# Norm's root and reciprocal on four rows instead of 128, spread by way of DRAM a slot later, its sum in another PSUM bank, and the x taps of the convolution a slot later

## The chip, the core and the metric

The kernel runs on one core of one Trainium2 chip. The metric is the device time of one execution in microseconds. The engines are named as in the profile: PE is TensorE (PEld its weight loads), DVE is VectorE, ACT is ScalarE, POOL is GpSimd, SP is SyncE, whose queue issues the DMAs.

## The reference, cut to what matters

A layer norm is followed by a Mamba-2 mixer and, beside it, a linear layer with mixture-of-LoRA; both are added to the input. There are 2048 tokens of 1024 features, 64 heads of 64 channels in 8 groups of 512 channels, and a state of 128. Everything is fp32. The change concerns the norm of the mixer (`var` and `yn`) and the convolution before it.

```python
proj = jnp.einsum('bld,pd->blp', hidden_states, in_proj_w)   # gate, hbc, dt
for k in range(K):                                           # K = 4
    conv = conv + pad[:, k:k + L, :] * conv_weight[:, k]
xBC = silu(conv)                                             # x, Bm, Cm
...                                                          # scan over tokens gives y
yg = y.reshape(B, L, G, GROUP_SIZE)                          # 8 groups of 512 channels
var = jnp.mean(yg * yg, axis=-1, keepdims=True)
yn = (yg * lax.rsqrt(var + EPS)).reshape(B, L, I) * norm_weight
yn = yn * silu(gate)
out = jnp.einsum('bli,di->bld', yn, out_proj_w)
```

## The kernel before, in words

Channels lie on the 128 partitions and tokens along the free axis. The work has two stages on one stream of instructions for each engine.

The first stage, up to about 2700 us, interleaves the input projections with the scan. A projection is computed in pairs of channel tiles by a Strassen-like scheme of seven products (`pair`, L450): product 1 goes to bank `pa`, 6 to `px`, 5 to `py`, then 2, 7, 3 and 4 add to them. Each product is four matmuls of 128x128 weights with 512 tokens, which the profile records as eight passes, since an fp32 matmul is two. DVE or ACT evicts what is finished (L474 to L482 and `stored`, L523): for a gate tile, ACT applies Silu to what DVE evicted (L533). Products of the x tiles are named ps_a_x, ps_x_x, ps_y_x in the profile, those of the gate ps_a_g and so on. In order they are here called products one to seven of a pair. The four banks of the pool `proj` hold them; the four banks `y`, `e`, `st` and `aux` (`ps_one`) hold everything else.

The scan is cut into 32 blocks (s, g, half): s is a half of 1024 tokens, g a group of 512 channels, half one of two runs of 512 tokens. A block has four slots c = 0 to 3 of 128 tokens. In each slot the main loop runs four or five products and, between them, what the scan needs:

- `scan_b` for this slot: ps_y (scores times `xdt`), ps_e (state times C), ps_st (the product that updates the state, from `xdd`); then on DVE ecp (L763), y (L764) and the state addition (L778), which needs POOL's multiplication of the state (L83).
- `scan_a` for the next slot, in three steps: the decay scan es on DVE (L688); ps_cb and a transpose into bank aux, copied by ACT (cbm, bt) and multiplied on DVE (dab, L702); four transposes ps_xt into bank aux, from which ACT makes eight pieces of `xdt` (L713) and eight of `xdd` (L721).
- `conv` for the next block in slots c = 1 and 2: ACT writes the first tap (L640), DVE adds three more taps for each of six tiles of 512 tokens (L646), first the two tiles `bc`, then the four tiles `xg`; ACT applies Silu (L653). `xg` has two buffers. The next block's `xg` takes the buffer of the block before this one, so it waits until that block's normed y has been stored.
- the norm of the block before, in slot c = 0: `norm_mean` sums the squares over channels with one matmul against a 128x128 tile of ones, so all 128 partitions hold the same sum; it writes bank aux (ps_nv) and ACT takes the root (L813). `norm_gate` takes the reciprocal (L819), scales four tiles by it (L822), multiplies them with the gate (L830), and SP stores them (y, L831). The squares come from `norm_squares` in slot c = 3 of the block itself.
- in the first half, `small`: the layer norm, the decays dt and the router of the second half's tokens, in small DVE steps (L311 to L395); `at` (L329) goes to an exp on ACT (L330).

The lists `parts[0]` to `parts[4]` spread side steps over the products of a slot. PE's order, the pieces of xdt and xdd, and Silu of the convolution are kept as written. The rest is put into each engine's queue by the framework's scheduler, so DVE's order differs from the order of the source. Each engine then runs its queue in order, and SP too: a DMA that waits holds up those behind it.

The second stage, from about 2742 us, is the output projection, in the same manner with two levels; the change does not touch it.

Of the kernel before, what the change touches and what calls it, by code (L numbers as in the profile page):

```python
# [8 lines left out]
F32 = mybir.dt.float32  # L9
AF = mybir.ActivationFunctionType  # L10
# [17 lines left out]
P = 128  # L28
TS = 1024
NS = L // TS  # L30
TB = 512
Q = 128
NQ = TB // Q
# [9 lines left out]
def mamba_lora_kernel(  # L43
# [17 lines left out]
    nc = tc.nc  # L61

    dram = ctx.enter_context(tc.tile_pool(name="dram", bufs=1, space=bass.MemoryType.DRAM))
    const = ctx.enter_context(tc.tile_pool(name="const", bufs=1))
# [6 lines left out]
    ps_one = ctx.enter_context(tc.tile_pool(name="ps_one", bufs=1, space=bass.MemoryType.PSUM))  # L71
    scan_ctx = ExitStack()
    p1 = scan_ctx.enter_context(tc.tile_pool(name="p1", bufs=1))
# [4 lines left out]
    def mm(*args, **kw):  # L78
        tc.keep_in_program_order(nc.tensor.matmul(*args, **kw))  # L79
# [11 lines left out]
    ones = const.tile([P, P], F32, name="ones")  # L91
    nc.vector.memset(ones, 1.0)
    ident = const.tile([P, P], F32, name="ident")
    make_identity(nc, ident)
    eps = const.tile([P, 1], F32, name="eps")
    nc.vector.memset(eps, EPS)


# [42 lines left out]
    nw = p1.tile([P, INNER // P], F32, name="nw")  # L141
# [151 lines left out]
    def small_mm(ps, x_of):  # L293
        for k in range(KT):
            mm(ps, x_of(k), wsm[:, k, :], start=(k == 0), stop=(k == KT - 1))
# [295 lines left out]
    def products(n, side):  # L591

        nonlocal done
        left = list(side)
        for i in range(n):
            next(stream)
            done += 1
            take = -(-len(left) // (n - i))
            for step in left[:take]:
                step()  # L600
            left = left[take:]
        for step in left:
            step()

    def steps(gen, n):

        return [lambda: next(gen, None) for _ in range(n)]


    xbc_of = {}  # L610
# [174 lines left out]
    def load_gate(s, g, half):  # L785
        sg = p1.tile([P, 4, TB], F32, tag="sg", name=f"sg_{s}_{g}_{half}")
        at = s * TS + half * TB
        nc.sync.dma_start(sg, gate_d[g][:, :, at : at + TB])
        sg_of[s, g, half] = sg

    norm_of = {}
# [14 lines left out]
        yield  # L806

    def norm_mean(s, g, half):
        y = y_of[s, g, half]
        ps = ps_one.tile([P, TB], F32, tag="aux", name=f"ps_nv_{s}_{g}_{half}")  # L810
        mm(ps, ones, y[:, 0, :], start=True, stop=True)
        std = p1.tile([P, TB], F32, tag="rms", name=f"rms_{s}_{g}_{half}")
        nc.scalar.activation(std, ps, AF.Sqrt, bias=eps, scale=1.0 / (4 * P))  # L813
        norm_of[s, g, half] = std

    def norm_gate(s, g, half):

        xg, std = xbc_of[s, g, half][0], norm_of[s, g, half]
        nc.vector.reciprocal(std, std)  # L819
        yield  # L820
        for j in range(4):
            nc.vector.scalar_tensor_tensor(  # L822
                xg[:, j, :], xg[:, j, :], nw[:, 4 * g + j : 4 * g + j + 1], std,
                ALU.mult, ALU.mult,
            )
        yield
        at = s * TS + half * TB
        for j in (0, 2):
            two = xg[:, j : j + 2, :]
            nc.vector.tensor_tensor(two, two, sg_of[s, g, half][:, j : j + 2, :], ALU.mult)  # L830
            nc.sync.dma_start(y_d[g][:, j : j + 2, at : at + TB], two)  # L831
            yield
# [121 lines left out]
    blocks = [(s, g, h) for s in range(NS) for g in range(G) for h in range(2)]  # L954
# [15 lines left out]
    def target(slot):  # L970
        for (s0, p0), (s1, p1_) in zip(plan, plan[1:]):
            if slot <= s1:
                return p0 + (p1_ - p0) * (slot - s0) // (s1 - s0)
# [4 lines left out]
    for b, blk in enumerate(blocks):  # L978
        s, g, half = blk
        prev = blocks[b - 1] if b else None  # L980
        nxt = blocks[b + 1] if b + 1 < len(blocks) else None

        i, stage = divmod(b - 2, 3)
        piece, after = (1, i), stage
        if not (s == 0 and 0 <= i < NQ):
            piece = after = None
        if b == 14:
            ln_ctx.close()
            wo_ctx = ExitStack()
            wo = wo_ctx.enter_context(tc.tile_pool(name="wo", bufs=1, reuse_waits="tile"))  # L990
        if b == 15:
            base_left = left_sums
        if 0 <= b - 15 < 16:
            left_sums = out_sums(wo, b - 15)
        for c in range(NQ):
            slot += 1
            n = target(slot) - done
            follow = (*blk, c + 1) if c + 1 < NQ else (*nxt, 0) if nxt else None
            second = (*blk, c + 2) if c + 2 < NQ else (*nxt, c + 2 - NQ) if nxt else None
            side = []  # L1000
            if c == 0 and nxt:
                side += [lambda: load_raw(*nxt)]
            if after == 0 and c == 1:
                load_piece(*piece, "sg", p1)
                ln = ln_next(*piece)
            if after == 0 and c == 2:
                side += steps(ln, 3)
            if after == 0 and c == 3:
                side += steps(ln, 4)
            if after == 1 and c in (0, 2, 3):  # L1010
                side += steps(rest, 1)
            if c in (1, 2) and nxt:
                if c == 1:
                    conv_steps = conv(*nxt)
                side += steps(conv_steps, 4)
            if c == 2 and after != 0:
                side += [lambda: load_gate(*blk)]
            if b == 1 and c < 2:

                js = range(4) if c == 0 else range(4, 7)  # L1020
                side[:0] = [
                    lambda j=j: nc.sync.dma_start(xop_d[0][j], ops_of["x", 0][j]) for j in js
                ]
            a = scan_a(*follow) if follow else iter(())
            parts = [side[i * len(side) // n : (i + 1) * len(side) // n] for i in range(n)]

            products(1, parts[0])
            if c == 0 and prev:
                norm_mean(*prev)
            scan_b(*blk, c)  # L1030
            if b == 14 and c:
                next(left_sums)
            if 0 <= b - 15 < 16 and c:
                next(left_sums)
            if second:
                load_decays(*second)
            next(a, None)
            if c == 0 and prev:
                out = norm_gate(*prev)
                parts[1:4] = [[*p, lambda: next(out, None)] for p in parts[1:4]]  # L1040
                parts[3] += [lambda: next(out, None)] * 2
            if c == NQ - 1:
                sq = norm_squares(*blk)
                parts[1] += steps(sq, 2)
                parts[2] += steps(sq, 1)
            products(1, parts[1])
            next(a, None)
            products(1, parts[2])
            products(1, parts[3])
            next(a, None)  # L1050
            if after == 0 and c == 1:
                next(ln)
            for i in range(4, n):
                products(1, parts[i])
            if b == 14:
                left_sums = base_sums(wo, c)
                next(left_sums)
            if 0 <= b - 15 < 16 and c == 0:
                if b == 15:
                    next(base_left)  # L1060
                next(left_sums)
            if after == 0 and c == 2:
                next(ln)
            if after == 0 and c == 3:
                sm = lp.tile([P, 2, NSM], F32, tag="sm", name=f"sm_{piece[0]}_{piece[1]}")
                ps = ps_one.tile([P, 2, NSM], F32, tag="st", name=f"ps_sm_{piece[1]}")
                for h in range(2):
                    small_mm(ps[:, h, :], lambda k: piece_of[piece][:, k, h, :])
                nc.scalar.copy(sm, ps)
                rest = small(*piece, slice(piece[1], 2 * NQ, NQ), sm, home)  # L1070
                load_gate(*blk)
            if (after, c) in ((1, 1), (2, 0)):
                next(rest)
    norm_mean(*blocks[-1])
    for _ in norm_gate(*blocks[-1]):
        pass
    wo_ctx.close()
# [156 lines left out]
    for t, (s, p) in enumerate(passes):  # L1234
        last = t + 1 == len(passes)
        for u, i in enumerate(units):
            ops, next_ops = next_ops, {}
            side = [[] for _ in range(7)]
# [87 lines left out]
            for n, j in enumerate(inner):  # L1326
                w = w_ready.pop(0)
                ps = {1: pa, 2: pa, 6: px, 7: px, 4: px, 5: py, 3: py}[j]
                for q in range(2):
                    for k in range(KH):  # L1330
                        mm(
                            ps[:, q, :], w[:, q, k, :], ops[j][:, k, :],
                            start=(n < 3 and q + k == 0), stop=(k == KH - 1), skip_group_check=True,
# [69 lines left out]
```

## Time and profile before

| what | us |
|---|---|
| time, median of 3 runs (3449.82 to 3451.58) | 3449.89 |
| the profiled execution's own time | 3453.59 |
| its span | 3451.8 |
| PE busy | 3409.2 |
| DVE busy | 2501.2 |
| ACT busy | 1164.7 |
| POOL busy | 696.1 |

The span runs from the first to the last instruction of the program in the profiled execution; 1.8 us of its own time lie around it. Busy time is a sum over all stages. A busy PE is not always a PE at its full rate: passes are pipelined, and a pass that starts late or runs at a lower clock counts as busy too. So the rate is read from the distance between starts of passes: 0.43 us for 512 columns, 0.109 for 128 columns (ps_xt). In the lines of groups and of the timeline, out<-in are the program's own names and x is a count; the bracket or the last column tells how long the engine sat idle just before and what ended it.

### The profile page before, as it was taken

Reading aid. Unit: us, or ns where it says so; the run is one execution under the profiler, and the core shown is the slowest. Engines: PE = TensorE matmul, PEld = TensorE weight load, DVE = VectorE, ACT = ScalarE, POOL = GpSimd, SP = SyncE. Lnnn points to the kernel's source line nnn. Section 1 sums busy time; section 2 is a strip of 40 time slices with the busy share of each in tenths; the row PEclk is TensorE's granted clock in tenths of the full one; section 3 lists DMA queues with packets and bytes.
Section 4 is the critical chain, followed back from the end, with each engine's and each line's share of the span. In section 5 each row is a group of like instructions: output and inputs, shape, how many; then the busy total and the mean of one; then the engine's idle time right before and its main releaser. Section 6 shows DMA issues by size and latency. Waiting matters only on the chain.

```text
span 3451.8 us, 38274 instructions
## 1 busy us (share of the span) xinstructions
PE 3409.2 (99%) x12818; PEld 1992.3 (58%) x12818; DVE 2501.2 (72%) x2861; ACT 1164.7 (34%) x3182; POOL 696.1 (20%) x443
## 2 busy tenths in 40 slices
PE   9999999999999999999999999999999999999999
PEld 7444544544545544454455445444444588888888
DVE  7548877877977877777787877777775466566665
ACT  2234453444444443444445444444442100000000
POOL 3122223222222211322223232222321000000000
PEclk9999999999999999999999999999999999999999
DMA  6546655655666676887778887777778687586654
GB/s 235 186 166 197 205 191 186 211 187 197 203 200 204 205 254 219 291 256 231 236 242 260 236 258 244 245 237 236 228 239 267 243 277 242 196 299 188 214 164 146
DMA packets 530324, 769.83 MB, mean 223 GB/s; under 512 B 35152, under 2 KB 264656, under 8 KB 527440
## 3 DMA queue, kind: packets, MB, share of 16 engines
q1 hardware_dynamic: 530128, 767.39, 68.7%
q8 instruction: 102, 1.67, 0.2%
q14 instruction: 94, 0.77, 0.1%
HBM read 516.64 MB, written 250.61 MB: 222 GB/s over the span
## 4 chain that ended last, share of the span: by engine, by line
PE 84%; DVE 9%; issue 3%; ACT 2%; DMA 1%; POOL 0%; SPq 0%; DVEq 0%; ACTq 0%; POOLq 0%
PE ps_x_x L79 12%; PE ps_x_w L79 8%; PE ps_a_x L79 8%; PE ps_y_x L79 8%; PE ps_x_g L79 7%; PE ps_a_w L79 6%; PE ps_y_w L79 6%; PE ps_y_g L79 5%; PE ps_a_g L79 4%; PE ps_y L79 3%; PE ps_e L79 3%; PE ps_st L79 2%; PE ps_x_b L79 2%; DVE xg L646 2%; PE ps_a_b L79 2%
## 5 line engine op out<-in xcount | busy, mean ns | idle before, releaser
L83 POOL TENSOR_TENSOR state<-state,tot 128x512 f32<-128x512 f32 x112 | 153.7, 1373 | 1326.0 <-PE ps_e L79 1199.8
L688 DVE TENSOR_TENSOR_SCAN es<-dab,here 128x1024 f32<-128x1024 f32 x128 | 304.6, 2380 | 83.4 <-ACT xdd L721 81.8
L646 DVE SCALAR_TENSOR_TENSOR xg<-rawx,cw,xg 128x512 f32<-128x512 f32 x384 | 339.2, 933 | 18.7 <-ACT xg L640 18.0
L79 PE MATMUL ps_x_w<-t,w 128*128 128x256 f32 x1344 | 303.8, 379 | 0.0
L713 ACT ACTIVATE xdt<-ps_xt,dt 128x64 f32<-128x64 f32 x1024 | 223.8, 333 | 209.7 <-PE ps_xt L88 209.7
L79 PEld LDWEIGHTS ps_x_w<-t,w 128*128 128x128 f32 x1344 | 255.4, 190 | 41.5 <-issue 7.7
L721 ACT ACTIVATE xdd<-xdt,es 128x64 f32<-128x64 f32 x1024 | 261.9, 388 | 0.0
L1340 ACT COPY s<-ps_a_w 128x512 f32<-128x512 f32 x28 | 16.4, 586 | 636.0 <-PE ps_a_w L79 555.5
L83 POOL TENSOR_TENSOR wo<-wo 128x512 f32<-128x512 f32 (+1 forms) x112 | 213.4, 1906 | 6.8
L79 PE MATMUL ps_a_w<-q,w 128*128 128x256 f32 x896 | 202.5, 379 | 0.0
L702 DVE TENSOR_TENSOR dab<-es,cbm 128x1024 f32<-128x1024 f32 x128 | 180.1, 1407 | 29.6 <-ACT cbm L698 29.6
L79 PEld LDWEIGHTS ps_a_w<-q,w 128*128 128x128 f32 x896 | 170.2, 190 | 23.6 <-issue 0.5
L79 PEld LDWEIGHTS ps_y<-dab,xdt 128*64 128x64 f32 x2048 | 114.6, 139 | 105.1 <-ACT xdd L721 38.7
L79 PE MATMUL ps_x_x<-op_again,s_x 128*128 128x512 f32 x384 | 172.7, 592 | 0.0
L79 PE MATMUL ps_y_x<-op_again,s_x 128*128 128x512 f32 x384 | 172.7, 592 | 0.0
L79 PE MATMUL ps_a_x<-op_again,a_x 128*128 128x512 f32 x384 | 172.7, 592 | 0.0
L79 PE MATMUL ps_x_x<-op,s_x 128*128 128x512 f32 x368 | 165.5, 592 | 0.0
L79 PE MATMUL ps_y_x<-op,s_x 128*128 128x512 f32 x368 | 165.5, 592 | 0.0
L79 PE MATMUL ps_a_x<-op,a_x 128*128 128x512 f32 x368 | 165.4, 592 | 0.0
L79 PE MATMUL ps_y<-dab,xdt 128*64 128x128 f32 x2048 | 146.6, 284 | 7.8 <-ACT xdt L713 7.8
L531 DVE TENSOR_TENSOR ev<-ps_x_x,s_x 128x512 f32<-128x512 f32 x94 | 64.5, 687 | 120.5 <-PE ps_x_x L79 116.1
L646 DVE SCALAR_TENSOR_TENSOR bc<-rawb,cw,bc 128x512 f32<-128x512 f32 x192 | 145.7, 790 | 1.9 <-ACT bc L640 1.0
(236 smaller groups left out, 6118.6 us busy)
## 6 DMA issues: line engine op xcount, KB each, us to landing
w<-w SPq DMA_DIRECT2D x196, 512.0 KB, 3.7
dab<-da_d SPq DMA_DIRECT2D x128, 512.0 KB, 5.5
raw<-ev SPq DMA_DIRECT2D x192, 256.0 KB, 3.3
a_x<-in_w_in_dram SPq DMA_DIRECT2D x168, 256.0 KB, 4.2
w<-wo SPq DMA_DIRECT2D x96, 448.0 KB, 4.3
ecp<-run_d SPq DMA_DIRECT2D x256, 128.0 KB, 4.0
gate<-ev SPq DMA_DIRECT2D x128, 256.0 KB, 3.9
sg<-gate SPq DMA_DIRECT2D x32, 1024.0 KB, 7.8
```

The source lines that it names most:

```text
L79: tc.keep_in_program_order(nc.tensor.matmul(*args, **kw))
L83: ins = nc.gpsimd.tensor_tensor(*args)
L531: nc.vector.tensor_tensor(e, ps, add, alu)
L646: nc.vector.scalar_tensor_tensor(dst[:, i, :], raw[:, i, k : k + TB], cw[:, ti, k : k + 1], dst[:, i, :], ALU.mult, ALU.add,)
L688: nc.vector.tensor_tensor_scan(es.rearrange("p h t -> p (h t)"), dab.rearrange("p h t -> p (h t)"), here, 0.0, ALU.mult, ALU.add,)
L702: nc.vector.tensor_tensor(ms, es, cbm.unsqueeze(1).to_broadcast([P, HG, Q]), ALU.mult)
L713: ins = nc.scalar.activation(xdt[:, h, :], x_t[:, h, :], AF.Copy, scale=dt_of[s][:, half * NQ + c, at : at + 1],)
L721: ins = nc.scalar.activation(xdd[:, h, :], xdt[:, h, :], AF.Copy, scale=es[:, h, Q - 1 : Q])
L1340: nc.scalar.copy(s1, pa)
```

## The change

- `norm_mean` sums into bank st instead of aux, with four matmuls instead of one. Each has 128 tokens, and as weights four columns of a new tile `row_of` [128, 8], which is zero but for column 3 (ones) and column 7 (EPS). Matmul c takes columns 3 - c to 6 - c, so its sums land in row c of a tile [4, 128], and the other three rows get zeros added. ACT takes the root of 4x128 instead of 128x512.
- A new step `norm_spread` takes the reciprocal of 4x128, stores it to DRAM, and loads it back with one DMA that copies the row of 512 to all 128 partitions.
- `norm_mean` moves behind `scan_b` and the second product of slot c = 0, `norm_spread` stands behind the third product, and `norm_gate` moves to slot c = 1.
- Of the convolution's steps, two instead of four stand in slot c = 1 (the tiles bc) and five instead of four in slot c = 2 (the tiles xg).
- After the last block the same steps follow each other with nothing between.

```diff
-    eps = const.tile([P, 1], F32, name="eps")
+    row_of = const.tile([P, 8], F32, name="row_of")
+    nc.vector.memset(row_of, 0.0)
+    nc.vector.memset(row_of[:, NQ - 1 : NQ], 1.0)
+    eps = row_of[:, 7:8]
     nc.vector.memset(eps, EPS)
...
     def norm_mean(s, g, half):
         y = y_of[s, g, half]
-        ps = ps_one.tile([P, TB], F32, tag="aux", name=f"ps_nv_{s}_{g}_{half}")
-        mm(ps, ones, y[:, 0, :], start=True, stop=True)
-        std = p1.tile([P, TB], F32, tag="rms", name=f"rms_{s}_{g}_{half}")
-        nc.scalar.activation(std, ps, AF.Sqrt, bias=eps, scale=1.0 / (4 * P))
-        norm_of[s, g, half] = std
+        n = f"{s}_{g}_{half}"
+        ps = ps_one.tile([NQ, Q], F32, tag="st", name=f"ps_nv_{n}")
+        for c in range(NQ):
+            mm(
+                ps, row_of[:, NQ - 1 - c : 2 * NQ - 1 - c], y[:, 0, c * Q : (c + 1) * Q],
+                start=(c == 0), stop=(c == NQ - 1),
+            )
+        rms = p1.tile([P, TB], F32, tag="rms", name=f"rms_{n}")
+        nc.scalar.activation(
+            rms[0:NQ, 0:Q], ps, AF.Sqrt, bias=eps[0:NQ], scale=1.0 / (4 * P)
+        )
+        norm_of[s, g, half] = rms
+
+    def norm_spread(s, g, half):
+        rms = norm_of[s, g, half]
+        std = rms[0:NQ, 0:Q]
+        n = f"{s}_{g}_{half}"
+        nc.vector.reciprocal(std, std)
+        std_d = dram.tile([NQ, Q], F32, tag=f"std_d_{n}", name=f"std_d_{n}")
+        nc.sync.dma_start(std_d, std)
+        nc.sync.dma_start(
+            rms, std_d.rearrange("c t -> (c t)").unsqueeze(0).to_broadcast([P, TB])
+        )

     def norm_gate(s, g, half):
-        xg, std = xbc_of[s, g, half][0], norm_of[s, g, half]
-        nc.vector.reciprocal(std, std)
-        yield
+        xg, rms = xbc_of[s, g, half][0], norm_of[s, g, half]
         for j in range(4):
             nc.vector.scalar_tensor_tensor(
-                xg[:, j, :], xg[:, j, :], nw[:, 4 * g + j : 4 * g + j + 1], std,
+                xg[:, j, :], xg[:, j, :], nw[:, 4 * g + j : 4 * g + j + 1], rms,
                 ALU.mult, ALU.mult,
             )
...
-                side += steps(conv_steps, 4)
+                side += steps(conv_steps, 2 if c == 1 else 5)
...
             products(1, parts[0])
-            if c == 0 and prev:
-                norm_mean(*prev)
             scan_b(*blk, c)
...
-            if c == 0 and prev:
+            if c == 1 and prev:
                 out = norm_gate(*prev)
-                parts[1:4] = [[*p, lambda: next(out, None)] for p in parts[1:4]]
-                parts[3] += [lambda: next(out, None)] * 2
+                for i in range(1, 4):
+                    parts[i] += steps(out, 1)
...
             products(1, parts[1])
+            if c == 0 and prev:
+                norm_mean(*prev)
             next(a, None)
             products(1, parts[2])
+            if c == 0 and prev:
+                norm_spread(*prev)
             products(1, parts[3])
...
     norm_mean(*blocks[-1])
+    norm_spread(*blocks[-1])
     for _ in norm_gate(*blocks[-1]):
         pass
```

## The prediction

> **What bounds the kernel now.** I read the page first (busy shares, slices, chain), then the list of what TensorE waits for, then the timeline around its longest wait, then busy time in the four slots of one block, and last the rows of the operations that change. From the page:
>
> ```profile
> span 3451.8 us, 38274 instructions
> PE 3409.2 (99%) x12818; PEld 1992.3 (58%) x12818; DVE 2501.2 (72%) x2861; ACT 1164.7 (34%) x3182; POOL 696.1 (20%) x443
> ```
>
> TensorE is the bound: 99% busy in every slice. So the change can win only what TensorE still waits for. Those waits, engine, line and cause, then us in total, times and longest:
>
> ```profile
> PE ps_nv L79 <- ACT xdt L713: 10.5, 4, 3.3
> PE ps_y L79 <- ACT xdt L713: 7.8, 5, 4.6
> ...
> PE ps_x_x L79 <- DVE ev L531: 2.8, 3, 1.3
> PE ps_x_g L79 <- DVE ev L531: 2.5, 5, 0.9
> ...
> PE ps_st L79 <- ACT xdd L721: 1.4, 4, 0.4
> ```
>
> All named waits sum to 37.3 us (1.1% of the span); the five shown make 25.0, and each lies in the scan, where the change works. A wait also costs what comes after it. The longest one (start, length, what, and in brackets the idle time before it):
>
> ```profile
> 443.47 3.60 PE L79 MATMUL ps_x_g<-op,s_g 128*128 128x512 f32 x8
> 451.65 2.17 PE L79 MATMUL ps_y<-dab,xdt 128*64 128x128 f32 x16 [4.58 <-ACT xdt L713]
> 453.75 1.76 PE L79 MATMUL ps_e<-bc,state 128*128 128x128 f32 x8
> 455.34 1.02 PE L79 MATMUL ps_st<-xdd,bt 128*128 128x512 f32 x2
> ```
>
> Elsewhere ps_y follows its product at once and goes to ps_e after 1.03 us, ps_e to ps_st after 0.97 (1552.33, 1553.36, 1554.35). Here it is 2.10 and 1.59: the clock granted between 451.65 and 455.34 was 0.54.
>
> Who is behind it? VectorE's queue. Busy time in slots c = 0 to 3 of block (1,4,1), one row each: window, its length, then PE, PEld, DVE, ACT, POOL:
>
> ```profile
> 2172.00:2192.00 20.00, 20.00 (x65) 9.63 (x65) 15.76 (x17) 7.91 (x24) 1.04 (x1) 1.00 0.53 168
> 2192.00:2210.00 18.00, 18.00 (x79) 9.28 (x73) 16.02 (x21) 9.17 (x26) 7.70 (x5) 1.00 0.71 218
> 2210.00:2228.00 18.00, 18.00 (x73) 9.29 (x69) 8.48 (x9) 5.82 (x21) 10.72 (x5) 1.00 1.01 328
> 2228.00:2246.00 18.00, 18.00 (x72) 9.37 (x71) 15.79 (x19) 10.64 (x26) 0.00 (x0) 1.00 0.85 249
> ```
>
> VectorE is 15.8 and 16.0 us busy in c = 0 and 1, 8.5 in c = 2, 15.8 in c = 3. An eviction that stands behind such a queue is late, ScalarE stands in order behind the eviction, xdt behind that, and TensorE behind xdt. The change empties c = 0 and fills c = 2.
>
> **What the Trainium skill says.** "TensorE: Matmul & The Clock Gate", Part 1: an array idle for about 3.4 us falls to half clock and needs as long to come back. The trace agrees: 0.54 granted after the 4.58 us wait. [...] the quickest stores here (s_b_d below) land after 2.0. "SBUF — State Buffer", Who interferes with whom: a VectorE instruction with two SBUF inputs contends with a GpSimd one that reads SBUF. The taps agree: 0.74 us alone, 1.75 beside GpSimd's work (1970 to 1973).
>
> **The change part by part.** Rows used (VectorE and ScalarE: ns min/median/max; DMA: KB and median us to landing):
>
> ```profile
> L822 DVE SCALAR_TENSOR_TENSOR xg<-xg,nw,rms x128: 736/745/1750, 270.1 to 2700.6; 128x512 f32<-128x512 f32 x128
> L813 ACT ACTIVATE rms<-ps_nv,eps x32: 687/687/689, 261.9 to 2694.5; 128x512 f32<-128x512 f32 x32
> L819 DVE RECIPROCAL rms<-rms x32: 3341/3346/3354, 264.0 to 2695.2; 128x512 f32<-128x512 f32 x32
> dab<-da_d SPq DMA_DIRECT2D x128, 512.0 KB, 5.5
> ecp<-run_d SPq DMA_DIRECT2D x256, 128.0 KB, 4.0
> s_b_d<-wb SPq DMA_DIRECT2D x16, 256.0 KB, 2.0
> ```
>
> 1. Reciprocal. 32 of 3.35 us go. The new one has 128 columns; 128x512 takes 3.35 and 128x256 1.75, so 6.25 ns a column gives 0.95. Saved: 32 x 2.4 = 77 us of VectorE, none of it on TensorE's path by itself. ScalarE's root falls from 0.69 to about 0.3 (cbm, 128 columns, takes 0.26), and 8 of 91 table loads (1.28 each) go by the new order: no path.
>
> 2. The sum on TensorE. Two passes of 512 columns, start to start 0.43 + 0.52 = 0.95 a block, become eight of 128 columns; ps_xt's, as long, start 0.109 apart: 0.87. Only four output rows are used, which no row shows. Bounds: 0.1 less each (-3 us in all) to 0.2 more (+6; ps_y and ps_e pay some 0.2 between them when the array's shape changes). I take +1.
>
> 3. The sum moves behind the state product and a projection product, from bank aux to bank st. Before, it needed aux, so all eight xdt; now ps_y comes first and needs only the first xdt, and ps_st all eight xdd. Where it waited, ps_st can start 0.1 after xdd's end, less the 0.95 that the sum then costs later:
>  - wait at 1573.15: xdd ends 1574.98, ps_st began 1577.65: 2.67 - 0.1 - 0.95 = 1.6;
>  - at 2168.03 and 2471.99: 2.83 - 1.05 = 1.8 each;
>  - at 2320.52: 1.25 - 1.05 = 0.2.
>  Sum 5.4 us. The other 27 blocks had no such wait and gain nothing.
>  New wait: the sum on bank st needs the state addition (L778) to have read ps_st. Before, the reciprocal stood ahead of it, typically 0.81 to 4.15 us after ps_st began, the addition ending at 5.3. In the changed order it follows ecp directly: it ends 1.5 us after the old place of ps_st, the sum comes at -0.95 + 0.86 + 3.44 = 3.35. Margin 1.8; least where es ends late (0.9). Only block (0,2,1), with ecp at 3.2, misses it: 1 us. Behind a waiting sum stand ps_cb and the next product. GpSimd's order is unchanged, and its state multiplication ends by 2.0.
>
> 4. The small head's steps. In four slots (waits at 446, 701, 951, 1199) ScalarE's exp of `at` stands ahead of xdt, and `at` behind the reciprocal, four scalings (0.75) and two gate products (1.22): 8.8 us. In the new order at (L329) stands ahead of all scaling. From the product's last pass to ps_st takes 2.52 when undisturbed; it took 8.86, 4.97, 4.58 and 4.97. Gain 6.3 + 2.45 + 2.05 + 2.45 = 13.3 us. Next late there would be the eviction of product five, which now follows the scaling; it has two products of room.
>
> 5. Taps (L646) a slot later. In the new order four of the eight evictions that TensorE waited for stand ahead of the taps; the waits at 1607 (1.1), 1974 (1.5), 2350 (0.85) and 2507 (1.1 and 1.1 behind it) go: 5.6 us. 2126 has one tap more ahead of it: +0.7.
>  Cost: VectorE in c = 2 rises from 8.5 by eight to twelve taps (0.74 to 1.75): 15 to 20 of 18 us; c = 0 falls to about 8, c = 1 to about 13. In c = 3 there are 2 us of room. I take 4 us of new late evictions; bounds 0 and 40.
>
> 6. The way through DRAM. SP gets 64 more issues (0.35 each), and the load waits for the store: behind it stand weight loads and ev's stores, for up to 2 us a block. SP has idle stretches (2181.3 to 2184.4), weights come a pair of products ahead: nothing. Trip: store 2.2, issue, load between ecp's and dab's, 4.5: rms is there 9.8 us after the sum began. VectorE stands in order before the first scaling for some 3 us, then needs 5.4 for it. In seven blocks the eviction of product five is behind that and is due 18.9 after the sum began: 9.8 + 5.4 + 0.7 = 15.9 is in time. I take 2 us; bounds 0 and 25. The convolution's first step waits for y's store (3.1) to free xg; it had 20 us of room.
>
> 7. The end. The last block's scaling has no slot to move into: the trip ends scaling some 3 us later (2706.8), and the s_b_2 eviction behind it is due 2708.0. I take 0.5; bounds 0 and 3.
>
> Sum: 5.4 + 13.3 + 5.6 = 24.3 won; 1 + 1 + 0.7 + 4 + 2 + 0.5 = 9.2 lost; -15 us. The profiled execution's own time is 3453.59: 3438.5. The median of the runs is 3.7 lower, and the waits are the same instructions there: 3449.9 - 15 = 3435.
>
> **Rivals.** (a) The waits only move: a full c = 2 gives as many late evictions as go. For it: DMA share 1.01 and GpSimd 10.7 us in that very slot. Lost 9 + 13: 3448. (b) Slower: VectorE becomes the bound in c = 2. With GpSimd at work a tap takes 1.75; if the twelve average over 1.0 us, they exceed c = 2's 9.5 and c = 3's 2 free us. At 1.25 they spill 3.5 us into the evictions at the end of c = 3, on which xdt waits; in 12 of the second half's 16 blocks that is 42 lost: 3449.9 - 24 + 5 + 42 = 3473; at 1.15 (2.3 us, 28 lost), 3459. Against: many taps are still placed in c = 1, which has 5 us of room. (c) No new waits: 3449.9 - 24.3 + 1.5 = 3427. (d) The row's load lands later than 7.5 us (state<-st, also a load of what was just stored, 7.4): product five's eviction late in seven blocks, +10: 3445.
>
> **Chances.** My forecast 0.58 (3427 to 3443), (a) and (d) 0.20, (b) 0.14, (c) 0.08. About 0.2% (7 us) is what measurement can tell from no change. Faster: 0.95 x 0.58 + 0.08 + 0.2 x 0.20 = 0.67; slower 0.13; same 0.20. The range leaves a tenth on each side: 3421 to 3457.
>
> **What would show it.** Right: the wait of ps_nv for xdt gone; no 446-like gap; reciprocals near 0.95 us; TensorE's named waits near 20 us. Wrong: ps_nv waiting for the state addition in many blocks, VectorE idle over 4 us before scaling, ps_y waiting for xdt at every c = 0, or VectorE over 17.5 us busy in c = 2 with taps at 1.75.

## The result, and the profile after

The changed kernel takes 3545.58 us (median of 5 runs, 3542.04 to 3550.89); the kernel before, on the same chip, 3451.58. The ratio is 1.0273, 95% interval 1.0258 to 1.0287: 94 us slower, where 15 us faster was forecast. From the page after:

```profile
span 3549.1 us, 38770 instructions
PE 3448.7 (97%) x13010; PEld 2012.0 (57%) x13010; DVE 2449.9 (69%) x2863; ACT 1140.2 (32%) x3174; POOL 715.4 (20%) x443
```

VectorE has 51 us less to do, as meant, and TensorE stands more. Its waits (engine, line and cause, then us in total, times, longest):

```profile
PE ps_y L79 <- ACT xdt L717: 21.9, 11, 4.8
PE ps_x_x L79 <- DVE ev L535: 19.5, 8, 5.1
PE ps_x_g L79 <- DVE ev L535: 15.8, 7, 6.2
PE ps_mean L79 <- DVE half L187: 13.6, 4, 4.2
...
PE ps_st L79 <- ACT xdd L725: 2.9, 8, 0.4
...
PE ps_nv L79 <- DVE state L782: 1.1, 2, 0.9
```

All named waits sum to 95.2 us, against 37.3 before. The waits of ps_nv for xdt are gone, and waits for evictions (ev, the second and third line) have taken far more than their place: 5.3 us before, 35.3 after. The waits for xdt at ps_y rose too (7.8 before), and so did those of the layer norm's sum, ps_mean, for a step of VectorE (1.4 before). The waits make 57.9 of the 97.3 us between the two profiled executions. The other 39 us are in TensorE's busy time (3409.2 before): its mean granted clock is 0.990 against 0.997, and after the waits it runs slower, 0.93 in the stretch from 1825.0 to 1843.5. Estimated from the mean clocks and the two spans, the lower clock makes some 25 of the 39 us; what makes the rest is open.

Why are the evictions late? VectorE itself stands. Its two longest new waits:

```profile
DVE xg L844 <- DMA rms<-std_d: 93.0, 27, 9.8
DVE xg L650 <- ACT xg L644: 92.7, 27, 10.7
```

The first is the scaling, waiting for the row from DRAM. The second is the convolution's taps, waiting for ScalarE's first step on the same x rows. And that step waits for something else:

```profile
ACT xg L644 <- DMA y<-xg: 175.6, 25, 12.9
```

It writes the tile from which the norm's product of the block before is still being stored. The same two waits in the kernel before:

```profile
DVE xg L646 <- ACT xg L640: 18.0, 8, 11.0
ACT xg L640 <- DMA y<-xg: 29.5, 11, 7.9
```

So there are two suspects: the trip of the row, and the store of the product. Here is the longest of TensorE's waits, seen as a piece of the chain of work (start us, us, what):

```profile
1731.98 3.45 PE ps_y_g L79 x8
...
1735.46 0.70 DVE s_g L486
1736.16 0.18 SPq L539
...
1736.44 0.38 SPq L427
...
1736.91 0.40 SPq L427
...
1737.36 5.87 DMA y<-xg
...
1743.33 0.82 ACT xg L644
...
1744.18 4.71 DVE xg L650 x5
```

The product had ended at 1726.83, but its store is issued at 1737.36 only: in SyncE's queue it stands behind an eviction's store (L539) and two weight loads (L427). It lands 5.87 us later, ScalarE starts, and VectorE, which has stood 5.84 us at the taps, does ten of them and three steps of the scan (ecp, state, y) before it comes to the eviction of ps_x_g at 1754.52. TensorE waits for that one for 6.22 us. SyncE's queue ahead of the store (start, length, what):

```profile
1720.11 0.37 SPq L853 DMA_DIRECT2D y<-xg  x1
1720.71 0.32 SPq L539 DMA_DIRECT2D raw<-ev  x1
1721.12 0.74 SPq L669 DMA_DIRECT2D dab<-da_d  x1
1730.19 2.16 SPq L893 DMA_DIRECT2D w<-wo  x3
1732.45 3.22 SPq L677 DMA_DIRECT2D ecp<-run_d  x2
1735.76 0.58 SPq L539 DMA_DIRECT2D raw<-ev  x1
1736.44 0.87 SPq L427 DMA_DIRECT2D s_g<-s_g_d  x2
1737.36 0.46 SPq L853 DMA_DIRECT2D y<-xg  x1
```

The first half of y went out at once (1720.11). Between the halves SyncE stood until 1730.19 for weights that GpSimd makes (w from wo, L893). On average over the 30 blocks whose tile a later convolution overwrites, the second store is issued 5.16 us after its product (at most 17.5); before it was 0.20. The two halves of the product, back to back before, now lie 2.67 us apart, with the next chunk's steps between them. The landing takes no longer (4.3 us where a convolution waited for it, 5.2 before).

The trip, in the same trace, where VectorE stands longest for it:

```profile
1467.60 0.93 DVE L833 RECIPROCAL rms<-rms 4x128 f32<-4x128 f32 x1
1468.46 1.47 DVE L706 TENSOR_TENSOR dab<-es,cbm 128x1024 f32<-128x1024 f32 x1
1470.95 0.69 DVE L486 TENSOR_TENSOR s_x<-ps_y_x,s_x 128x512 f32<-128x512 f32 x1 [1.03 <-PE ps_y_x L79]
1481.45 6.78 DVE L844 SCALAR_TENSOR_TENSOR xg<-xg,nw,rms 128x512 f32<-128x512 f32 x4 [9.81 <-DMA rms<-std_d]
1488.16 1.21 DVE L852 TENSOR_TENSOR xg<-xg,sg 128x1024 f32<-128x1024 f32 x1
1489.30 0.68 DVE L535 TENSOR_TENSOR ev<-ps_x_x,s_x 128x512 f32<-128x512 f32 x1
```

VectorE stands 9.81 us, then scales for 6.78 (beside GpSimd, 1.75 each), and TensorE waits 5.07 us for the eviction behind.

### The profile page after: what moved, and what is told of

The parts are those of the page before. It is cut to its first block, busy times and chain, and to the rows that moved or that the text cites. A ratio compares the mean times of both kernels' runs of the same rounds, so it can differ in the third digit from the quotient of the medians.

```text
span 3549.1 us, 38770 instructions
## 1 busy us (share of the span) xinstructions
PE 3448.7 (97%) x13010; PEld 2012.0 (57%) x13010; DVE 2449.9 (69%) x2863; ACT 1140.2 (32%) x3174; POOL 715.4 (20%) x443
## 4 chain that ended last, share of the span: by engine, by line
PE 74%; DVE 11%; DMA 6%; issue 4%; ACT 3%; POOL 1%; SPq 1%; DVEq 0%; ACTq 0%; POOLq 0%
PE ps_x_x L79 11%; PE ps_x_w L79 8%; PE ps_a_x L79 7%; PE ps_y_x L79 6%; PE ps_x_g L79 6%; PE ps_y_w L79 5%; PE ps_a_w L79 5%; PE ps_a_g L79 4%; PE ps_y_g L79 3%; DVE xg L650 3%; PE ps_y L79 3%; PE ps_e L79 3%; DMA y<-xg 2%; PE ps_x_b L79 2%; PE ps_st L79 2%
## 5 line engine op out<-in xcount | busy, mean ns | idle before, releaser
L83 POOL TENSOR_TENSOR state<-state,tot 128x512 f32<-128x512 f32 x112 | 169.9, 1517 | 1350.5 <-PE ps_e L79 1146.9
L650 DVE SCALAR_TENSOR_TENSOR xg<-rawx,cw,xg 128x512 f32<-128x512 f32 x384 | 325.3, 893 | 101.3 <-ACT xg L644 92.7
L83 POOL TENSOR_TENSOR wo<-wo 128x512 f32<-128x512 f32 (+1 forms) x112 | 228.5, 2040 | 6.8
L706 DVE TENSOR_TENSOR dab<-es,cbm 128x1024 f32<-128x1024 f32 x128 | 176.5, 1379 | 14.9 <-ACT cbm L702 14.9
L79 PEld LDWEIGHTS ps_a_w<-q,w 128*128 128x128 f32 x896 | 170.2, 190 | 23.6 <-issue 0.5
L844 DVE SCALAR_TENSOR_TENSOR xg<-xg,nw,rms 128x512 f32<-128x512 f32 x128 | 106.1, 889 | 93.0 <-DMA rms<-std_d 93.0
L644 ACT ACTIVATE xg<-rawx,cb,cw 128x512 f32<-128x512 f32 x128 | 95.3, 807 | 198.6 <-DMA y<-xg 175.6
```

Of the source, the lines that this page charges most:

```text
L83: ins = nc.gpsimd.tensor_tensor(*args)
L644: nc.scalar.activation(dst[:, i, :], raw[:, i, 0:TB], AF.Identity, bias=cb[:, ti : ti + 1], scale=cw[:, ti, 0:1],)
L650: nc.vector.scalar_tensor_tensor(dst[:, i, :], raw[:, i, k : k + TB], cw[:, ti, k : k + 1], dst[:, i, :], ALU.mult, ALU.add,)
L706: nc.vector.tensor_tensor(ms, es, cbm.unsqueeze(1).to_broadcast([P, HG, Q]), ALU.mult)
L844: nc.vector.scalar_tensor_tensor(xg[:, j, :], xg[:, j, :], nw[:, 4 * g + j : 4 * g + j + 1], rms, ALU.mult, ALU.mult,)
```

## The experiments

Each run shares its chip with runs of the kernel before (3450.5 to 3451.1 in these sets). The edits are shown as diffs.

**First set: which of the suspects.** The product stored from another tile, so that the convolution doesn't wait for the landing:

```
-            nc.vector.tensor_tensor(two, two, sg_of[s, g, half][:, j : j + 2, :], ALU.mult)
-            nc.sync.dma_start(y_d[g][:, j : j + 2, at : at + TB], two)
+            out = sg_of[s, g, half][:, j : j + 2, :]
+            nc.vector.tensor_tensor(out, two, out, ALU.mult)
+            nc.sync.dma_start(y_d[g][:, j : j + 2, at : at + TB], out)
```

> The changed kernel, with the gate product written into the gate's own tile and stored from there, so that the convolution's first step on the x rows needs only the product read, not its store landed. Theory S (store): the next block's convolution writes the tile that the norm's product is stored from; with the norm in slot c = 1 and the x taps at the start of c = 2, ScalarE waits for the store (175.6 us in the trace after, 29.5 before), VectorE's taps stand behind it (92.7 us), and 63 of the 118 us of TensorE's gaps lead back to it. S expects those ScalarE waits near zero and 50 to 70 us back: 3475 to 3495. Theory Q (VectorE's queue in c = 2 is too full of taps): nothing comes back, 3535 to 3550. Theory T (the row's trip through DRAM holds VectorE, 93.0 us idle): 3530 to 3550.

Measured: 3498.31 us, ratio 1.0139 (1.0124 to 1.0154): 47 us back, just under the 50 to 70 of theory S. ScalarE no longer waits for a store, and the taps stand 23.6 us for ScalarE. Of the waits that remained, VectorE's for the row is the large one:

```profile
DVE xg L844 <- DMA rms<-std_d: 84.5, 25, 10.3
```

No trip, with the sum, root and reciprocal of before on 128 rows at the new places (this gives VectorE its long reciprocals back as well):

```
+        ps = ps_one.tile([P, TB], F32, tag="st", name=f"ps_nv_{s}_{g}_{half}")
+        mm(ps, ones, y[:, 0, :], start=True, stop=True)
...
     def norm_spread(s, g, half):
...
+        std = norm_of[s, g, half]
         nc.vector.reciprocal(std, std)
...
-        nc.sync.dma_start(std_d, std)
-        nc.sync.dma_start(
-            rms, std_d.rearrange("c t -> (c t)").unsqueeze(0).to_broadcast([P, TB])
-        )
```

> The changed kernel with the sum of before (128 equal rows of 512, root and reciprocal over all of them) at the new places; no trip through DRAM, all else as changed. Theory T: the 93.0 us that VectorE stands before the scaling are what was lost, so most of it comes back: 3470 or less. Theory S: 12 us of TensorE's gaps lead back to the trip, and scaling up to 3 us earlier gets the store out a little earlier: 3515 to 3535, with ScalarE's waits for the store still over 120 us. Theory Q: 77 us more of VectorE, none of it in c = 2: 3545 or slower.

Measured: 3474.88, ratio 1.0074 (1.0059 to 1.0089): 71 us back, near what theory T expected and more than twice what S did, although VectorE had 59 us more to do. Theory S alone falls. T alone does too: 24 us of loss remain, and ScalarE still waits 98.1 us for the store.

The convolution later in c = 2:

```
-                side += steps(conv_steps, 2 if c == 1 else 5)
+                side += steps(conv_steps, 2) if c == 1 else steps(iter(()), 2) + steps(conv_steps, 5)
```

> The changed kernel with the convolution's steps in slot c = 2 two places later (two empty steps ahead of them), so that the x rows are first written some 7 us later in the slot. Theory S: most stores have landed by then, 30 to 60 us back: 3485 to 3515. Theory Q: the taps crowd together at the end of c = 2 and run into c = 3, slower than the changed kernel: 3550 to 3580. Theory T: no change, 3545.

Measured: 3536.97, ratio 1.0253 (1.0238 to 1.0268). ScalarE's wait for the store is 175.5 us, as it was: the edit moved the lines of the source, but the scheduler left the convolution where it was. Of a block's twelve taps on x rows 5.4 start in c = 1 and 5.8 in c = 2 in the changed kernel, 5.5 and 5.8 in this run (means of 32 blocks, a slot counted from one ps_y to the next). Inconclusive.

The taps alone, in the kernel before:

```
-                side += steps(conv_steps, 4)
+                side += steps(conv_steps, 2 if c == 1 else 5)
```

> The kernel before with the convolution's split alone changed (two steps in c = 1, five in c = 2): the norm stays in c = 0. Theory S: the store has landed a slot before, the taps move at little cost: 3440 to 3465. Theory Q: the full c = 2 was the loss, 3490 to 3550. Theory T: 3450.

Measured: 3453.00, ratio 1.0007 (1.0000 to 1.0014). The edit of the lists costs nothing that stands clear of the noise, but it is no test of theory Q, for it did not fill c = 2. In the kernel before 11.0 of the twelve taps start in c = 1, in this run as well, and VectorE is 9.4 and 9.3 us busy in c = 2. In the changed kernel, where 5.8 of them start in c = 2, it is 14.3; with the product stored from the gate's tile 10.3 are back in c = 1, and it is 10.7. So it is the late store, not this edit, that fills c = 2. How much of the 47 us came from an emptier c = 2 and how much from ScalarE's wait is not separated.

**Second set: do the two suspects explain all of it?** Both edits at once:

> The changed kernel with both edits at once: the sum of before over 128 equal rows at the new places (no trip), and the product stored from the gate's tile. The first runs gave 71 us back for the trip and 47 for the store. Theory ST (one chain: the trip makes the scaling late, the late scaling makes product and store late, the store holds the convolution): the two overlap, and together they are all of the loss of 95 us: 3447 to 3460, ScalarE waits for no store, VectorE for no row. Theory Add (two separate losses, and the moves of sum and taps win what was forecast): 3425 to 3440. Theory Rest (a third loss besides them, such as the taps in c = 2 beside GpSimd): 3465 or slower.

Measured: 3448.88, ratio 0.9992 (0.9983 to 1.0000). As theory ST had it: the two edits would give 118 us if they added, and give 97, so they overlap, and the kernel is as fast as before. ScalarE waits for no store and VectorE for no row.

The trip a product earlier in the source (and, in the second kernel, the store from the gate's tile as well):

```
             if c == 0 and prev:
                 norm_mean(*prev)
+                norm_spread(*prev)
             next(a, None)
             products(1, parts[2])
-            if c == 0 and prev:
-                norm_spread(*prev)
```

> The changed kernel with the reciprocal and the trip issued right after the sum, one projection product (3.4 us) earlier; same instructions, same traffic. Theory ST: what counts is the row's arrival against the scaling, so the 93 us that VectorE stands before the scaling fall to 30 or less and 30 to 60 us come back: 3485 to 3515. Rival Traffic (64 more issues and their waits in SyncE's queue are what costs, whenever they come): 3535 to 3550.

> The trip one product earlier and the product stored from the gate's tile, everything else as changed. Theory ST: nearly everything comes back, 3450 to 3470. Rival Traffic: as with the store from the gate's tile alone, 3490 to 3505.

Measured: 3541.45 (ratio 1.0257, 1.0241 to 1.0272) and 3499.76 (1.0140, 1.0125 to 1.0155). By their numbers theory ST would fall, but the traces show that there was no test: the reciprocal ends 3.35 us after the sum's start (median) in the changed kernel and in this one, and the load is issued at 6.17 in both. The trip had been about as early already. Rival Traffic falls with the next run, which has the same 64 issues.

The norm back in c = 0, with trip and taps as changed. Sum and trip go to the sum's old place and bank; then:

```
-            if c == 1 and prev:
+            if c == 0 and prev:
                 out = norm_gate(*prev)
-                for i in range(1, 4):
-                    parts[i] += steps(out, 1)
+                parts[3] += steps(out, 3)
```

> The changed kernel with the norm back in slot c = 0: the four-row sum at its old place ahead of the state products and in bank aux, reciprocal and trip right after it, scaling, product and stores after the fourth product of c = 0; the taps stay as changed. Theory ST: the stores have landed long before the convolution (ScalarE waits for them under 40 us), the row arrives with some 7 us of products more in hand: 3445 to 3465. Rival Trip (the trip costs by itself wherever it is, through VectorE's stand before the scaling): VectorE over 80 us idle there and 3475 to 3500.

Measured: 3455.38, ratio 1.0013 (1.0004 to 1.0022), as theory ST said, though ScalarE waits 51.2 us for stores, not under 40. VectorE stands 61.6 us for the row, and the kernel is 2.4 us slower than with the taps alone, which is within the two intervals. So a stand of VectorE is not a loss in itself.

**Third set: place of the sum, slot of the norm, queue of the store.** The changed kernel with the sum and trip alone at the old place:

```
             products(1, parts[0])
+            if c == 0 and prev:
+                norm_mean(*prev)
+                norm_spread(*prev)
             scan_b(*blk, c)
...
-        ps = ps_one.tile([NQ, Q], F32, tag="st", name=f"ps_nv_{n}")
+        ps = ps_one.tile([NQ, Q], F32, tag="aux", name=f"ps_nv_{n}")
```

> The changed kernel with only the sum, its reciprocal and its trip put back to the sum's old place and bank (ahead of the state products of c = 0, bank aux); the scaling is still written in c = 1 and the taps are split as changed. Theory Place (the sum's later place, 6.7 us, and the trip together make the scaling late; the scheduler puts the scaling where the row is ready, not where it is written): scaling, product and stores stand in VectorE's and SyncE's queues where they stood before, 3448 to 3462. Theory Slot (writing the norm in c = 1 is what puts its stores behind the weights' stores that wait for GpSimd): 3475 or slower.

Measured: 3464.06, ratio 1.0042 (1.0027 to 1.0057), between the two theories and close to Place: 81 of the 95 us come back with the place of sum and trip alone.

The sum alone moved, in the kernel before (not shown: its bank changes from aux to st). The norm's other steps start one product later, since they need the sum:

```
-            if c == 0 and prev:
-                norm_mean(*prev)
             scan_b(*blk, c)
...
-                parts[1:4] = [[*p, lambda: next(out, None)] for p in parts[1:4]]
-                parts[3] += [lambda: next(out, None)] * 2
+                parts[2:4] = [[*p, lambda: next(out, None)] for p in parts[2:4]]
+                parts[3] += [lambda: next(out, None)] * 3
...
             products(1, parts[1])
+            if c == 0 and prev:
+                norm_mean(*prev)
```

> The kernel before with the sum alone moved behind the second projection product of c = 0 and into bank st; root and reciprocal over 128 rows as before, norm in c = 0 and taps as before. Forecast of step 3: the waits of the sum for xdt go, 3445. Theory Place: the scaling comes 4 to 5 us later, the convolution's first x step stands behind the store, as in the run without a trip: 3460 to 3490, with ScalarE waiting over 80 us for the store.

Measured: 3436.83, ratio 0.9962 (0.9947 to 0.9976). Faster than both kernels, and theory Place is refuted: ScalarE waits over 80 us for the store, as it said, and TensorE does not feel it. ScalarE's wait, and then TensorE's:

```profile
ACT xg L640 <- DMA y<-xg: 121.2, 27, 9.4
```


```profile
PE ps_y L79 <- ACT xdt L713: 10.3, 6, 3.4
...
PE ps_x_x L79 <- DVE ev L531: 1.2, 4, 0.4
...
PE ps_x_g L79 <- DVE ev L531: 0.9, 3, 0.4
PE ps_nv L79 <- DVE state L778: 0.6, 1, 0.6
```

TensorE's waits sum to 24.4 us. Here the second store follows its product after 0.69 us and the taps stand 28.3 us.

The stores of the changed kernel on another queue:

```
-            nc.sync.dma_start(y_d[g][:, j : j + 2, at : at + TB], two)
+            nc.scalar.dma_start(y_d[g][:, j : j + 2, at : at + TB], two)
```

> The changed kernel with the two stores of the product issued on ScalarE's queue in place of SyncE's. In the trace after, the second store is issued 5.16 us after its product on average (up to 17.5), before 0.20, while the landing takes as long as before (4.3 against 5.2). Theory Queue (what stands ahead of the store in SyncE's queue is a main part): the issue follows the product at once, 20 to 40 us back, 3505 to 3525. Rival: ScalarE then stands for the product itself and xdt is late behind it, 3545 or slower.

Measured: 3494.89, ratio 1.0129 (1.0112 to 1.0146). The second store is issued 0.05 us after its product, and 51 us come back, more than theory Queue said and about as many as with the store from another tile (47). ScalarE's wait for the store is hardly shorter, 170.3 us, but the convolution starts 4.4 us after the product, where it started 9.7 after it (means of 30 blocks), and 9.2 of the twelve taps are back in c = 1. So what the store costs is mostly its place in SyncE's queue. Whether part of the 51 us comes from DMAs that no longer stand behind the store there is not separated.

The sum at its old place and the store from the gate's tile:

> The sum at its old place with the four-row root, reciprocal and trip, and the product stored from the gate's tile. Theory Place: nothing waits for store or row on TensorE's path, and 77 us less VectorE work is left as the only difference from before, off the path: 3440 to 3453. If the forecast's gains for steps 4 and 5 exist, 3430 to 3440.

Measured: 3457.67, ratio 1.0021 (1.0013 to 1.0030), a miss upward by 5 us: VectorE still stands 57.1 us for the row. No gain from the 77 us of reciprocal that VectorE is spared shows in the time.

**Fourth set: the norm's slot by itself.** The changed kernel with only the norm's writing back in c = 0:

```
-            if c == 1 and prev:
-                out = norm_gate(*prev)
-                for i in range(1, 4):
-                    parts[i] += steps(out, 1)
...
                 norm_spread(*prev)
+                out = norm_gate(*prev)
+                parts[3] += steps(out, 3)
             products(1, parts[3])
```

> The changed kernel with scaling, product and stores written at the end of slot c = 0, right after the trip, in place of c = 1; four-row sum at its new place, trip and taps as changed. Theory Slot (the later writing puts the product's second half behind the next chunk's work in VectorE's queue, and its store behind others in SyncE's): second store issued within 1 us of its product, and most of the loss gone, 3440 to 3460. Theory Trip (the row's arrival 10.8 us after a late sum is enough to make the evictions late): VectorE's idle time before the scaling stays over 80 us and 3485 to 3510.

Measured: 3482.61, ratio 1.0089 (1.0071 to 1.0108): 63 us back, 2.4 us below the range of theory Trip and 22.6 above that of theory Slot: both the slot and the trip cost. The second store is issued 0.12 us after its product, the halves lie together, and the two waits read:

```profile
DVE xg L844 <- DMA rms<-std_d: 88.4, 26, 11.0
...
DVE xg L650 <- ACT xg L644: 15.4, 5, 10.8
```

The sum moved and the taps later; and the sum moved with the store from the gate's tile:

> The kernel before with the sum moved (the run that gave 3437) and the taps split as changed; norm in c = 0, 128 rows, no trip. It stands one step from the run without a trip (3475), which has besides this the norm written in c = 1. If the norm's slot is what costs those 38 us: 3435 to 3445. If the taps cost once the sum is late: 3460 to 3475.

> The sum moved alone and the product stored from the gate's tile. The run with the sum alone still has ScalarE waiting 121 us for the store, but TensorE's gaps lead back to the store in 2.6 us only: 3430 to 3438. If that wait did cost elsewhere: 3420 to 3430.

Measured: 3439.86 (0.9971, 0.9960 to 0.9982) and 3439.83 (0.9968, 0.9955 to 0.9981). The first is as expected if the slot costs; its 3 us over the run with the sum alone are within the intervals, and here too the taps stayed in c = 1 (10.7 of twelve). The second is 2 us above the range. The store from another tile gains nothing where the store is issued in time, so ScalarE's 121 us were free.

Put side by side, all with the lists of the taps as changed (the corner left out was not run). Where the trip is "yes", sum, root and reciprocal are on four rows; where it is "no", on 128:

| sum | trip | norm written in | us |
|---|---|---|---|
| old place | no | c = 0 | 3453.0 |
| old place | yes | c = 0 | 3455.4 |
| old place | yes | c = 1 | 3464.1 |
| new place | no | c = 0 | 3439.9 |
| new place | no | c = 1 | 3474.9 |
| new place | yes | c = 0 | 3482.6 |
| new place | yes | c = 1 | 3545.6 |

With the sum at its old place the trip costs 2 us, which is not clear of the noise, and the later slot 9 more. With the sum later, the trip costs 43, the slot 35, and both 106.

## Why the prediction was wrong

By its own steps:

1. Reciprocal: right in its row, 0.94 us (0.95 forecast), and no gain from it shows in the time. The saving comes from fewer columns, not from fewer rows: in the kernel before a reciprocal of 128x128 takes 0.95 us too (L318). VectorE's busy time fell by 51 us, not 77: the scalings took 889 ns in the mean against 775, the products with the gate 1379 against 1217. The root took 0.36 (0.3 forecast). The rows after:

```profile
L823 ACT ACTIVATE rms<-ps_nv,row_of x32: 357/358/358, 266.1 to 2791.6; 4x128 f32<-4x128 f32 x32
L833 DVE RECIPROCAL rms<-rms x32: 930/941/942, 266.7 to 2792.0; 4x128 f32<-4x128 f32 x32
```

2. The sum's form on TensorE: within its bounds. The passes of ps_nv take 30.9 us start to start in all, against 31.9 before.

3 and 4. The sum's place, and with it the small head's exp: right in the mechanism, and the size was near. Together they were to give 18.7 us less a few; the sum moved alone gives 14.0 (3450.8 to 3436.8; by the interval, 8 to 18). The gaps at 701, 951 and 1199 are gone in that run, but the one at 446, for which 6.3 of the 13.3 us of step 4 were forecast, shrank only from 4.58 to 3.42. Of the waits for xdt at c = 0, 1573 fell from 3.27 to 1.83, 2168 from 2.11 to 0.68 and 2320 from 2.45 to 1.01, while the one at 2472 stayed (2.69 and 2.97). The waits for evictions at 1607, 1974, 2350 and 2507, which step 5 had counted for the taps, went in this run. The new wait on the state addition is small, 0.6 to 1.1 us in all, as said.

5. Taps: forecast 5.6 won and 4.7 lost. The edit by itself moved nearly nothing: its 2 to 3 us of loss are not clear of the noise, the taps stayed in c = 1, and the four waits for evictions that it was to remove are all there in the run with the taps alone. "The change empties c = 0 and fills c = 2" came true in the mean of the 32 blocks of the changed kernel, where VectorE is 11.6 us busy in c = 0 (15.7 before) and 14.3 in c = 2 (9.4 before), but through the late store. It did not happen in the block that the prediction showed, one of five in 30 in which ScalarE does not wait for the store. Its four slots after, in the columns of before (window, length, PE, PEld, VectorE, ScalarE, GpSimd):

```profile
2256.00:2276.00 20.00, 20.00 (x72) 9.37 (x70) 14.55 (x16) 7.43 (x23) 0.00 (x0) 1.00 0.49 159
2276.00:2294.00 18.00, 18.00 (x73) 9.29 (x70) 17.50 (x22) 9.57 (x26) 7.07 (x5) 1.00 0.72 218
2294.00:2312.00 18.00, 18.00 (x72) 9.37 (x71) 9.75 (x9) 6.45 (x21) 10.80 (x5) 1.00 1.00 320
2312.00:2330.00 18.00, 18.00 (x69) 9.13 (x68) 15.83 (x20) 9.94 (x25) 1.11 (x1) 1.00 0.98 285
```

VectorE is 9.75 us busy in c = 2 (8.48 before) and 17.50 in c = 1: here the store came in time, and the taps stand in c = 1 (2279.20 to 2292.20) as before. Rival (b), a full c = 2, had the right sign. C = 2 did get fuller, but because the store was late, which (b) does not have; what a fuller c = 2 costs by itself no run shows.

6. The way through DRAM is the step that failed. "Rms is there 9.8 us after the sum began" was nearly right: the scaling begins 10.8 us after it (median; 17.6 at most), and VectorE stands 2.9 us a block (93.0 in 32 blocks), where 3 was forecast. But "I take 2 us; bounds 0 and 25" is mis-sized by far: with the sum at its new place the trip costs 43 us with the norm in c = 0. With the sum at its old place the same trip costs 2.4. The old sum begins 6.3 us earlier (the three state steps 2.86, a product 3.44). Counted from that old place, the scaling begins after 9.6 us in the kernel before, 11.4 with the trip at the old place, 14.1 with the sum alone late, and 17.4 with both (means of 32 blocks). The times are 3450.8, 3455.4, 3436.8 and 3482.6 us, so either delay fitted, and both together did not. The prediction moved the sum later in step 3, and added the trip in step 6 against a room of "15.9 against 18.9", 3 us, from medians. The stand varies by block up to 9.8 us, and the scaling behind it by up to 4 us with GpSimd beside it.

And a sentence in the same step was false: "The convolution's first step waits for y's store (3.1) to free xg; it had 20 us of room." The trace of before does not show 20 us. ScalarE starts the convolution 5.2 us after the product on average and 0.9 us after the store has landed; in 11 of 30 blocks it already waits for the store. The change wrote product and store into c = 1. SyncE's queue then holds the second store for 5.2 us on average (6.4 in the run without the trip), VectorE's queue splits the product, and the taps behind it slip into c = 2. The later slot costs 35 us without the trip and 63 with it. The prediction priced 64 new issues in SyncE's queue, but did not ask where the 64 old ones, the stores of y, would stand after the move.

7. The end was not tested apart. In the trace after, the last block's scaling begins 8.3 us after its sum, 5.2 before: some 3 us later, as forecast.

So won 14, lost 3 (taps), 43 (trip behind a late sum) and 63 (the norm's slot behind a late row): 3450.8 - 14.0 + 3.0 + 42.7 + 63.0 = 3545.5. These are steps from one measured kernel to the next, so they add up by themselves; the 3 us of the taps are within the noise. That trip and slot cost 28 us more together than apart, with the sum late, is measured. That it is because one room is used up by all three delays is argued from the traces. Whether the old sum with the norm in c = 1 and no trip would cost anything was not tried.

## What to carry to other kernels

A step that makes a result later is priced against the room that is left after the other steps of the same change, not against the room of the kernel before: here the late sum alone won 14 us and the trip alone cost about 2, but trip and later slot behind a late sum cost 106. When a step that ends in a store is moved, look for who overwrites the stored tile next, and for what stands ahead of the store in its queue at the new place. An edit of the source is a test only if the trace shows that the engine's queue has changed: in four of these runs (the convolution later, the taps alone, and the two with the earlier trip) what was to move hardly moved. The part worth keeping was the simplest one, the sum moved behind a product (3436.8 us, 0.9962 of before).

## What the runs showed of the hardware

Of two long waits of an in-order engine, neither tells its cost by its length. ScalarE's wait for the store was 121 us in the run with the sum alone and 140 in the changed kernel with the norm in c = 0, and taking it away in the first gained nothing. VectorE's stand for the row was 61.6 us in a run 2.4 us slower than without it, and 88.4 in one that was 43 slower. The waits that TensorE itself shows did follow the time in order in these four: 24.4 us in the fastest kernel, 37.3 before, 48.5 with the norm in c = 0, 95.2 after (3436.8, 3450.8, 3482.6 and 3545.6 us). They are less than the loss, 57.9 us of 97.3 between the profiled executions of before and after; part of the rest is the lower clock behind them.

A wait's length alone does not tell whether the clock falls, so the 3.4 us of the prediction is no sharp limit here. In the trace of before a wait of 2.11 us (until 2168.03) was followed by a granted clock of 0.59 up to 2172.20, and one of 2.45 us (until 2320.52) by 1.00 up to 2324.50.
